# Two attention stages of a two-layer kernel rewritten: rotated state columns, sums on TensorE, roots by logarithm, named activation tables, fewer filling matmuls, new buffers and a new order

## The chip, the core and the metric

The kernel runs on one core of one Trainium2 chip. The engines are called PE (TensorE; PEld is its weight load), DVE (VectorE), ACT (ScalarE), POOL (GpSimd) and SP (SyncE, here only an issuer of DMAs). The metric is the device time of one execution in microseconds (us); the median of several runs is compared.

## What is computed

Two transformer layers in float32 over 8 x 512 tokens of width 128. Each layer is an attention of a recurrent kind and a mixture of experts; each has a layer norm ahead of it and a residual around it.

```python
# layer 0: state per head (16 heads of 8), for every token
kk = kt[..., :, None] * kt[..., None, :]
state = state * (1.0 - bb * kk) + bb * (vt[..., :, None] * kt[..., None, :])
out_t = jnp.einsum('bhij,bhj->bhi', state, qt)     # q and k have length 1
...
logits = relu(x @ rw1 + rb1) @ rw2 + rb2           # 8 experts, top 2, at most 512 tokens each
# layer 1: gated linear attention (16 heads, keys of 4, values of 8)
gk = log_sigmoid(h @ gk_w1 @ gk_w2 + gk_b2) / 16
S = exp(gt)[..., None] * S + kt[..., None] * vt[..., None, :]
o = _rms(einsum('bhk,bhkv->bhv', qt, S), rms_w) * (g * sigmoid(g))
x = x + o @ Wo; x = x + gelu(_ln(x) @ W1 + b1) @ W2 + b2
...                                                # 16 experts, top 4, all tokens kept
```

## The kernel before, in words

The work comes in five stages, in the profile one after the other: **attention 0** (0 to 396 us), **experts 0** (to 480), **attention 1** (to 826), **experts 1** (to 1035) and the **output**.

The 8 sequences of 512 tokens are the batches b. A recurrence is run by DVE as a prefix scan along the tokens: 128 partitions are (head, row of the state), and one instruction scans four columns of the state, 128 x 2048 elements. Attention 0 has 8 columns, so two scans (groups g = 0 and 1) for a batch; attention 1 has 4 columns, one scan.

`attend0(b)` (L440) normalizes x (`affine`, L412, with a square root on ACT and a reciprocal on DVE, `statistics`, L423), transposes it on PE, projects it to keys, queries, values and gate, finds the norms of the heads by squares and a matmul (L584 to L600), and scales keys, queries and values. Keys and queries go to DRAM through SP's queue (L551, L557) and come back spread over the partitions, four columns for a transfer of 1 MB (`broadcasts`, L470, also on SP): `add` tiles for the keys, `qb` for the queries. Then for each group (L639 on): DVE multiplies keys by the row's key (`dec`, L643, 128 x 2048), ACT turns that into 1 - kk (`decay`, L621, L623), DVE multiplies by the value (L649), scans (L655) and multiplies by the queries (L659); PE sums the columns and centres them (`summing`, L626, L632, 8 matmuls of 512 columns for a batch). A root and a reciprocal (`deviation`, L673), the gate and the output projection follow. `route(b)` (L713) finds the two experts of each token and scatters the token's row to DRAM, one indirect DMA of POOL per 128 tokens and choice (L836). `fills` (L852) clears the DRAM areas, `later_constants` (L877) loads the expert weights `ew1_all` and `ew2_all` on SP during the whole stage.

`attend(b)` (L1080) is the like for layer 1: the two expert results are added to x on DVE (L1095), statistics and two roots (L1101, L1102), projections; keys and queries go out as `pairs` (L1160), the decays as `decays` (L1218), and `spread_rows` (L1140) brings them back as `kb`, `qb_both` and `gb_both`. The decay is exp((min(z,0) - ln(1 + exp(-|z|))) / 16), made by ACT with three table changes and by DVE (L1203 to L1215). A scan (L1232), a product with the queries, 16 matmuls that sum and transpose (L1245), a root mean square (L1253 to L1258), the gate, the output matrix, a second layer norm and an MLP with GELU follow. `residual` (L1108) adds the bias b2 to x on POOL (L1117). `route1(b)` (L1327) picks 4 of 16 experts and scatters each token four times (L1449, 16 indirect DMAs for a batch).

Experts 1 works on 144 tiles of 128 rows in 36 quads of four: `fetch` (L1583) loads the rows on SP, `prepare` (L1590) transposes them on PE and copies the expert's first weights out of `fw1` with an address read from a register (DVE, L1599), `first` (L1602) and `second` (L1619) are the two matmuls with GELU between; `second` reads the weights of `fw2` with an address read by PE (L1628). POOL scatters each tile (L1638). The output adds the four results of a token (L1674, L1676).

The order inside both attention stages is made by a small planner when the program is written (`Order`, L93 to L166): each batch is a set of chains that say which engine they want next and for how long, each with a rank (its batch; the routes get `b + BEHIND`); the planner takes the step that can begin first, then the lower rank. Tiles come from rings with a number of buffers (L332 on), a chain waits until one is given back. On the chip each engine then runs its instructions strictly in the planned order. Where the planner sees PE idle for longer than `FILL` (0.35), it puts in filling matmuls of 128 columns that write to a bank nobody reads (`fill`, L896, L898), one for each 0.35 us. A switch of the activation table is planned as 1.3 us; the loads themselves are put in by the builder.

Of the kernel before, what the change touches and what calls it, by code (L numbers as in the profile page):

```python
# [17 lines left out]
P = 128  # L18
B = 8
# [19 lines left out]
NC1 = I1 // P  # L39

# [22 lines left out]
PE, DVE, ACT, POOL, SP = "PE", "DVE", "ACT", "POOL", "SP"  # L63
HOP = 0.2
SWITCH = 1.3
FILL = 0.35
# [25 lines left out]

class Order:  # L93
# [6 lines left out]
    def __init__(self):  # L100
        self.engines = {}
        self.table = None
        self.fill = None
        self.chains = []
        self.now = 0.0
# [14 lines left out]
    def settle(self):  # L120
        moved = True
        while moved:
            moved = False
            for c in sorted(self.chains, key=lambda c: c[:2]):
                want = c[5]
                if isinstance(want, Signal):
# [17 lines left out]
    def run(self):  # L144
        self.settle()
        while self.chains:
            best = None
            for c in self.chains:
# [6 lines left out]
                switch = len(want) > 2 and self.table not in want[2].split("|")  # L155
                key = (start + (SWITCH if switch else 0.0), c[0], c[1])
                if best is None or key < best[0]:
                    best = key, c, engine, us, want[2].split("|")[0] if switch else self.table
            assert best is not None, "chains wait for each other"
            key, c, engine, us, self.table = best  # L160
            gap = key[0] - self.engines.get(engine, 0.0)
            if engine == PE and self.fill is not None and gap > FILL:
                self.fill(int(gap / FILL))
            c[2] = self.engines[engine] = key[0] + us
# [6 lines left out]
def two_layers(ctx: ExitStack, tc: tile.TileContext, a: dict, out: bass.AP):  # L171
# [7 lines left out]
    stage = ExitStack()  # L179

# [8 lines left out]
    def load(name, shape, src, queue=nc.gpsimd):  # L189
        t = const.tile(shape, F32, name=name)  # L190
        queue.dma_start(t, src)
        return t
# [6 lines left out]
    wk0 = load("wk0", [P, C], a["L0_attn_Wk"], nc.scalar)  # L199
    wq0 = load("wq0", [P, C], a["L0_attn_Wq"], nc.scalar)  # L200
    wb0 = load("wb0", [P, NH], a["L0_attn_Wbeta"], nc.scalar)
    wv0 = load("wv0", [P, C], a["L0_attn_Wv"], nc.scalar)
    wg0 = load("wg0", [P, C], a["L0_attn_Wg"], nc.scalar)
# [15 lines left out]
    center = const.tile([P, P], F32, name="center")  # L219
    nc.vector.tensor_scalar_add(center, ident, -1.0 / C)  # L220

    head_sum = const.tile([P, NH], F32, name="head_sum")
    nc.vector.tensor_reduce(head_sum, ident.rearrange("p (h d) -> p h d", d=D), AX.X, ALU.add)
    spread = const.tile([3 * NH, 3, P], F32, name="spread")
    for i in range(3):
# [4 lines left out]
        )  # L230
    number1 = const.tile([P, E1], F32, name="number1")
# [7 lines left out]
    first0 = const.tile([P, E0], F32, name="first0")  # L239
# [22 lines left out]
    wout0 = load("wout0", [P, C], a["L0_attn_Wout"])  # L262
    rw1 = load("rw1", [P, H0], a["L0_ffn_rw1"])
    rw2 = load("rw2", [P, NC0, E0], a["L0_ffn_rw2"].rearrange("(c p) e -> p c e", p=P))
    rb2 = load("rb2", [P, E0], a["L0_ffn_rb2"].partition_broadcast(P))
# [10 lines left out]
    ps = bank_ring.idle[0][2]  # L276
    nc.tensor.transpose(ps[:, :NCOLS], rows, ident[:NCOLS, :NCOLS])
    nc.vector.tensor_copy(cols, ps[:, :NCOLS])

    def col(at, n=P):  # L280
        return cols[:n, at : at + 1]


    wout_g = const.tile([P, C], F32, name="wout_g")
    nc.vector.tensor_scalar_mul(wout_g, wout0, col(LNG0))
    wout_b = const.tile([P, C], F32, name="wout_b")
    nc.vector.tensor_scalar_mul(wout_b, wout0, col(LNB0))
    rmsw2 = const.tile([P, 1], F32, name="rmsw2")
    nc.vector.tensor_scalar_mul(rmsw2, col(RMSW), 0.5)
# [5 lines left out]
    nc.vector.memset(empty, 0.0)  # L295
    nc.gpsimd.iota(
        empty[:, :, DEST : DEST + 1].bitcast(I32), [[0, 1], [0, 1]], base=NA0, channel_multiplier=0
    )
# [3 lines left out]
    zeros = const.tile([P, 2 * C], F32, name="zeros")  # L302
# [8 lines left out]
    ew1_all = experts.tile([P, E0, H0], F32, tag="first", name="ew1_all")  # L311
# [34 lines left out]
    h_ring = ring(work, 1, [P, NC0, S], "hT")  # L346
    pick = [P, NT, 2, E0]
    FLIGHT0 = 4
    BEHIND = 2
    finished = [0]  # L350

    class Small0:
# [1364 lines left out]
```

## Time and profile before

| what | us |
|---|---|
| median of 3 runs | 1061.47 (1058.1 to 1071.24) |
| the profiled execution | 1068.49 |
| its span, first to last instruction | 1066.7 |
| first scan of attention 0, last one | 51.5, 343.8 |
| first scan of attention 1, last one | 538.9, 720.6 |
| first scatter of attention 1, last one's start | 626.6, 822.5 |
| scatters of experts 1 | 841.3 to 1028 |
| mean granted PE clock | 0.854 |

A timeline line gives start and length in us, engine, line, operation, output<-inputs and shape; in brackets the idle time of the engine ahead of it and what ended it. A line of stretches gives start:end, length, then for PE, PEld, DVE, ACT and POOL the busy time and instructions, the granted PE clock, the busy share of the DMA engines and GB/s. A line of groups gives line, engine, operation, tiles and count, then busy time in us and mean in ns, then idle time ahead. A float32 matmul leaves two PE records; counts of matmuls in the text are counts in the program.

### The profile page before, as it was taken

To read this page: it belongs to the slowest core of one execution; us is meant where nothing else is said; L and a number is where in the kernel's file an instruction comes from. 1 tells how busy PE (TensorE), PEld (TensorE's weight loads), DVE (VectorE), ACT (ScalarE), POOL (GpSimd) and SP (SyncE) were. 2 spreads that over 40 slices of the span, in tenths; PEclk is the share of its full clock that TensorE was granted. 3 is DMA by queue.
4 is the path that set the end of the run, shared out by engine and by line. 5 is a ranking of instruction groups with operands and counts; after the bars stand their busy time and mean duration, and the time that the engine had idled before them with its cause. 6 is when DMAs were issued, how large, how long until landed. Compare 5 with 4: busy or idle time off the path is not lost. (4 is left out here: it accounts for less than half of the span.)

```text
span 1066.7 us, 15813 instructions
## 1 busy us (share of the span) xinstructions
PE 824.1 (77%) x4783; PEld 632.3 (59%) x4783; DVE 648.2 (61%) x1553; ACT 472.3 (44%) x900; POOL 475.5 (45%) x459
## 2 busy tenths in 40 slices
PE   6989799999888949987658986797880899888500
PEld 5756566666655734463557664677770899777400
DVE  5477886876897511118379987697552465544217
ACT  3734464473424403426424785454630455444200
POOL 9000013612316441542000138887776377777753
PEclk8887997886988968998869997889995899999855
DMA  7965854867533002016774447642511344432138
GB/s 173 229 150 128 197 141 116 199 181 189 148 84 92 5 9 78 22 49 170 191 174 108 113 121 182 157 117 66 180 52 50 91 126 119 119 98 78 51 126 272
DMA packets 81684, 132.08 MB, mean 124 GB/s; under 512 B 13044, under 2 KB 58998, under 8 KB 74432
## 3 DMA queue, kind: packets, MB, share of 16 engines
q1 hardware_dynamic: 61824, 100.86, 37.7%
q0 software_dynamic: 14832, 27.84, 9.1%
q10 hardware_dynamic: 4944, 2.37, 0.8%
q8 instruction: 39, 0.64, 0.3%
q14 instruction: 45, 0.37, 0.1%
HBM read 94.79 MB, written 41.14 MB: 127 GB/s over the span
## 5 line engine op out<-in xcount | busy, mean ns | idle before, releaser
L836 POOL DMA_INDIRECT row<-rows,si x64 | 91.2, 1426 | 270.6 <-DVE kT L614 148.9
L1449 POOL DMA_INDIRECT rows<-rows,si x128 | 151.9, 1187 | 57.1 <-issue 33.6
L1638 POOL DMA_INDIRECT res<-qy,to x144 | 143.2, 994 | 61.4 <-issue 33.6
L898 PE MATMUL idle_bank<-ones,ident 128*128 128x128 f32 x1216 | 166.9, 294 | 2.3 <-POOL ident masks.py:199 1.5
L898 PEld LDWEIGHTS idle_bank<-ones,ident 128*128 128x128 f32 x1216 | 159.1, 209 | 13.3 <-issue 10.2
L1617 ACT ACTIVATE qh<-mid,cols 128x128 f32<-128x128 f32 x288 | 85.9, 367 | 78.1 <-PE mid L1609 69.9
L1609 PE MATMUL mid<-dT,qw 128*128 128x128 f32 x576 | 73.2, 281 | 18.4 <-DVE dT L1600 18.4
L632 PE MATMUL acc<-add,center 128*128 128x512 f32 x128 | 67.3, 674 | 21.7 <-DVE add L659 21.4
L1609 PEld LDWEIGHTS mid<-dT,qw 128*128 128x128 f32 x576 | 68.3, 194 | 23.1 <-DVE dT L1600 23.1
L655 DVE TENSOR_TENSOR_SCAN add<-dec,add 128x2048 f32<-128x2048 f32 x16 | 70.8, 4424 | 0.6
L1628 PE MATMUL qyp<-fw,qh 128*128 x576 | 71.0, 276 | 0.0
L1117 POOL TENSOR_TENSOR x<-x,b 128x512 f32<-128x512 f32 x8 | 11.8, 1480 | 127.0 <-DVE u L1112 100.7
L1628 PEld LDWEIGHTS qyp<-fw,qh 128*128 128x128 f32 x576 | 67.5, 192 | 0.6 <-issue 0.2
L1599 DVE COPY qw<-fw 128x256 f32 x144 | 45.1, 315 | 34.4 <-DMA rows<-rows,si 17.8
L632 PEld LDWEIGHTS acc<-add,center 128*128 128x128 f32 x128 | 26.3, 216 | 53.6 <-issue 28.4
L1245 PE MATMUL acc<-ident,kb 128*128 128x128 f32 x256 | 35.1, 303 | 23.3 <-DVE gb_both L1230 21.7
L955 POOL DMA_INDIRECT res<-y,de x32 | 31.0, 969 | 46.9 <-DVE dT L928 22.0
L659 DVE TENSOR_TENSOR add<-add,qb 128x2048 f32<-128x2048 f32 x16 | 36.6, 2288 | 22.6 <-DMA qb<-queries 22.3
L1245 PEld LDWEIGHTS acc<-ident,kb 128*128 128x128 f32 x256 | 34.0, 218 | 24.1 <-DVE gb_both L1230 21.9
L623 ACT ACTIVATE dec<-dec 128x2048 f32<-128x2048 f32 x16 | 30.5, 1908 | 28.8 <-DVE dec L643 28.8
L1594 PE MATMUL qT<-ident,de 128*128 128x128 f32 x144 | 24.2, 284 | 23.0 <-DMA de<-rows 23.0
L1635 DVE TENSOR_TENSOR to<-de,nowhere 128x4 int32<-128x4 int32 x36 | 5.9, 163 | 58.7 <-DMA res<-qy,to 55.1
(335 smaller groups left out, 1752.5 us busy)
## 6 DMA issues: line engine op xcount, KB each, us to landing
add<-keys SPq DMA_DIRECT2D x16, 1024.0 KB
qb<-queries SPq DMA_DIRECT2D x16, 1024.0 KB
de<-rows SPq DMA_DIRECT2D x144, 65.0 KB
kb<-pairs SPq DMA_DIRECT2D x8, 1024.0 KB
qb_both<-pairs SPq DMA_DIRECT2D x8, 1024.0 KB
gb_both<-decays SPq DMA_DIRECT2D x8, 1024.0 KB
yk<-res SPq DMA_DIRECT2D x8, 1024.0 KB
res<-zeros POOLq DMA_DIRECT2D x8, 512.0 KB
```

The costliest lines, as they stand in the source:

```text
L632: nc.tensor.matmul(acc, lhsT=center, rhs=st[:, j, :], start=g + j == 0, stop=(g + 1) * J + j == D + J - 1)
L655: nc.vector.tensor_tensor_scan(flat, dec.rearrange("p j t -> p (j t)"), flat, 0.0, ALU.mult, ALU.add)
L659: nc.vector.tensor_mul(st, st, q_j)
L836: nc.gpsimd.indirect_dma_start(out=row0_w[(b * NT + t) * 2 + k], out_offset=bass.IndirectOffsetOnAxis(ap=m.si[:, t, k : k + 1], axis=0), i ...
L898: nc.tensor.matmul(idle_bank[:, 0:P], lhsT=ident, rhs=ones, start=True, stop=True)
L1245: nc.tensor.matmul(chunk(acc, t), lhsT=chunk(st[:, j, :], t), rhs=ident, start=j + t == 0, stop=j + t == DK + NT - 2)
L1449: nc.gpsimd.indirect_dma_start(out=rows1_w[(b * NT + t) * K1 + k], out_offset=bass.IndirectOffsetOnAxis(ap=m.si[:, t, k : k + 1], axis=0), ...
L1599: nc.vector.tensor_copy(w1_q[:, i, :], fw1[:, bass.ds(at, I1)])
L1609: nc.tensor.matmul(mid[c][:, here], lhsT=w1_q[:, i, c * P : (c + 1) * P], rhs=dT[:, here], start=True, stop=True)
L1617: nc.scalar.activation(hT[:, c, here], mid[c][:, here], AF.Gelu, bias=cols[:, bass.ds(at + c, 1)])
L1628: nc.tensor.matmul(ps[:, here], lhsT=hT[:, c, here], rhs=fw2[:, bass.ds(at + c * C, C)], start=c == 0, stop=c == NC1 - 1,)
L1638: nc.gpsimd.indirect_dma_start(out=res1_w[4 * q + i], out_offset=bass.IndirectOffsetOnAxis(ap=to[:, i : i + 1], axis=0), in_=y[:, i, :], i ...
```

## The change

It touches both attention stages, experts 1 and the planner.

- Attention 0, state columns: each tile of keys is written to DRAM twice, one after the other for each head, so that a partition (head, i) can read the four columns from column i + 4g on, wrapping round. The decay 1 - k_i k_c is symmetric, so three of the four decays of group 1 are those of group 0 in other rows: PE moves them with the permutation matrices `turned` and ACT copies them; DVE multiplies only one column of group 1 (512 elements instead of 2048). Queries are written and read in the same way.
- Roots: 1 / sqrt(v + eps) is now exp(-0.5 ln(v + eps)) on ACT (`inverse_root`), without a reciprocal on DVE, everywhere in both stages.
- Tables: steps name a whole table set (`EXP`, `GELU`, `SILU`), and the planner puts in the load itself (`order.load`).
- Sums on PE: in attention 1 the additions of expert results, of u, of b2 and of the two halves of the decay become matmuls with the identity that add up in PSUM, and the statistics read PSUM; ACT copies the sums to SBUF. POOL no longer adds b2. The rows for the scatter are normalized once and then copied four times per 128 tokens, into six small buffers where there were two of a whole batch.
- Stores of keys, queries, pairs and decays are issued by ACT, not SP. In attention 1 the queries' broadcast is issued behind that of the decays.
- Fillings: only for planned gaps of over 2.5 us, one wide matmul (512 columns, zeros) per us: 29 in the program, where there were 608 narrow ones.
- Buffers in attention 0: `add` 4 (3), `dec` 3 (2), `qb` 4 (2). The `qb` buffers take the room of the expert weights, which are therefore loaded after the last scan. The fills of DRAM begin after the first scan. The matrix of constants is transposed later. In attention 1 there are 4 banks (5) and 3 sums (2).
- Order: ranks are lists of numbers (`TURN0`, `REST0`, `ROUTE0`, `TURN`, `TURN_REST`, `TURN_ROUTE`), a batch changes its rank after its scan, and the planned lengths of steps are changed.
- Experts 1: the biases of the first layer lie beside the expert's weights, and DVE also copies the second weights, so PE and ACT read no addresses there; one of four row loads is issued by ACT.

The activation table loads in the built program are 24 in attention 0 (33 before), 38 in attention 1 (39), 1 in experts 1 (1).

The diff, cut to its core:

```diff
-FILL = 0.35
+FILL = 1.0
+PAUSE = 1.5
...
-            if engine == PE and self.fill is not None and gap > FILL:
-                self.fill(int(gap / FILL))
+            if table is not None:
+                self.table = table
+                self.load(table)
+            if engine == PE and self.fill is not None and gap > PAUSE + FILL:
+                self.fill(int((gap - PAUSE) / FILL))
...
+    order.load = nc.scalar.preload_act_table_set
-    a_ring = ring(work, 3, [P, J, S], "add")
-    d_ring = ring(work, 2, [P, J, S], "dec")
-    b_ring = ring(work, 2, [P, J, S], "qb")
+    a_ring = ring(work, 4, [P, J, S], "add")
+    d_ring = ring(work, 3, [P, J, S], "dec")
+    b_ring = Ring([t[:, i] for t in (qb_first, qb_second) for i in range(2)])
...
+    TURN0 = [-47.0, -20.5, -9.0, 3.5, 25.0, 10.0, 52.0, 111.0]
+    REST0 = [-12.0, -3.0, -100.0, -3.5, -74.0, 38.5, 21.5, -29.5]
+    ROUTE0 = [10.0, 12.5, 29.5, 55.0, 13.0, 46.0, 39.0, 42.0]
...
+    def inverse_root(dst, src, **of):
+        nc.scalar.activation(dst, src, AF.Ln, **of)
+        nc.scalar.activation(dst, dst, AF.Exp, scale=-0.5)
...
+                    bass.AP(every.tensor, every.offset + g * J * S, [[2 * D * S, NH], [S, D], [1, J * S]]),
...
+        def send(dst, src):
+            for r in range(2):
+                nc.scalar.dma_start(dst.rearrange("(h r j) t -> r h j t", r=2, j=D)[r], src)
...
-            nc.sync.dma_start(keys[b], kT)
+            send(keys[b], kT)
...
-        def decay(dec, done):
-            yield ACT, 1.93
-            nc.scalar.activation(dec, dec, AF.Identity, bias=1.0, scale=-1.0)
+        def decay(g, n):
+            yield ACT, 0.49 * n
+            nc.scalar.activation(decs[g][:, :n, :], decs[g][:, :n, :], AF.Identity, bias=1.0, scale=-1.0)
+            if g == 0:
+                decayed[0].set(order.now)
+                return
+            yield decayed[0]
+            for r in range(J - 1, 0, -1):
+                ps = yield bank_ring
+                yield PE, 0.93
+                nc.tensor.matmul(ps, lhsT=turned[:, r, :], rhs=decs[0][:, r, :], start=True, stop=True)
+                if r == 1:
+                    used_dec()
+                yield ACT, 0.6
+                nc.scalar.copy(decs[1][:, J - r, :], ps)
+                bank_ring.give(order.now, ps)
+            decayed[1].set(order.now)
...
-            yield DVE, 0.57 * J
-            nc.vector.tensor_mul(dec, st, by_j(kT))
+            n = J if g == 0 else 1
+            yield DVE, 0.57 * n
+            nc.vector.tensor_mul(dec[:, :n, :], st[:, :n, :], by_j(kT, n))
...
+    TURN = [-10.5, 6.0, 8.5, 11.5, 11.5, 16.0, 24.5, 10.0]
+    TURN_REST = [-35.5, -33.0, 6.5, 3.0, -73.0, -24.0, 81.0, 9.0]
+    TURN_ROUTE = [-7.5, -41.5, 1.0, -4.0, -17.0, 17.0, 8.5, -15.0]
...
-        for k in range(2):
-            yield DVE, 0.7
-            nc.vector.tensor_add(x_b, x_b, ys[:, :, k, :])
+        px = yield acc_ring
+        yield PE, 2.7
+        for i, part in enumerate((x_b, ys[:, :, 0, :], ys[:, :, 1, :])):
+            nc.tensor.matmul(tiled(px), lhsT=ident, rhs=part, start=i == 0, stop=i == 2)
...
-        yield ACT, 0.6, "sqrt"
-        nc.scalar.activation(m.rs["u"][:, 0, :], m.mv["u"][:, :, 1], AF.Sqrt, bias=eps)
-        nc.scalar.activation(m.rs["u"][:, 1, :], m.mv["u"][:, :, 1], AF.Sqrt, bias=eps2, scale=1.0 + EPS)
+        yield ACT, 0.8, EXP
+        inverse_root(m.rs["u"][:, 0, :], m.mv["u"][:, :, 1], bias=eps)
+        inverse_root(m.rs["u"][:, 1, :], m.mv["u"][:, :, 1], bias=eps2, scale=1.0 + EPS)
...
-            yield POOL, 1.3
-            nc.gpsimd.tensor_add(x_b, x_b, b2.unsqueeze(1).to_broadcast([P, NT, C]))
...
-            nc.sync.dma_start(pairs[b], kq)
+            nc.scalar.dma_start(pairs[b], kq)
...
+        for t in range(NT):
+            rw = yield rows_ring
+            yield ACT, 1.0
+            nc.scalar.copy(rw[:, :, 0:C], xr[:, t : t + 1, :].to_broadcast([P, K1, C]))
+            nc.scalar.copy(rw[:, :, WEIGHT], m.ex[:, t, :])
+            order.add(TURN_ROUTE[b], scatter(t, rw))
...
+            nc.vector.tensor_copy(w1_q[:, i, :], fw1[:, bass.ds(at, WE)])
+            nc.vector.tensor_copy(w2_q[:, i, :], fw2[:, bass.ds(at, I1)])
```

## The prediction

> **What bounds the kernel now.** I read the page's busy shares first, then the busy time of each engine in the five stages, the fillings alone, and then inside the two changed stages the timelines of POOL, DVE and ACT.
>
> ```profile
> span 1066.7 us, 15813 instructions
> PE 824.1 (77%) x4783; PEld 632.3 (59%) x4783; DVE 648.2 (61%) x1553; ACT 472.3 (44%) x900; POOL 475.5 (45%) x459
> ```
> No engine is full over the span, so the stages decide. Here they are (attention 0; experts 0; attention 1; experts 1; output); behind each stretch: its length, then busy time of PE, PEld, DVE, ACT, POOL, the granted clock, the DMA share, GB/s.
> ```profile
> 0.00:396.00 396.00, 343.50 (x1617) 239.72 (x1617) 280.38 (x585) 180.70 (x276) 122.89 (x131) 0.84 0.56 137
> 396.00:480.00 84.00, 75.08 (x276) 41.51 (x276) 10.49 (x16) 28.77 (x41) 31.36 (x33) 0.93 0.18 50
> 480.00:826.00 346.00, 250.95 (x1594) 204.07 (x1594) 241.99 (x678) 175.68 (x294) 165.01 (x144) 0.85 0.50 129
> 826.00:1035.00 209.00, 154.52 (x1296) 146.99 (x1296) 91.35 (x252) 87.19 (x289) 143.19 (x144) 0.91 0.35 95
> 1035.00:1067.00 32.00, 0.00 (x0) 0.00 (x0) 23.99 (x24) 0.00 (x0) 13.05 (x8) 0.50 0.84 283
> ```
> The same for the filling matmuls alone (PE, PEld): 69 of the 343 us and 89 of the 251 us of PE are fillings, so real PE work is 275 and 162 us.
> ```profile
> 0.00:396.00 396.00, 68.69 (x478) 65.36 (x478) 0.84 0.56 137
> 480.00:826.00 346.00, 88.60 (x654) 84.33 (x654) 0.85 0.50 129
> ```
> In attention 0 DVE sets the pace: 280 us of work, and what stops it is a transfer or another engine for a few us at a time, such as the queries here. In attention 1 the first half is a chain of small waits; DVE, in order, even stands behind a store that SP issued late:
> ```profile
> 64.27 2.29 DVE L659 TENSOR_TENSOR add<-add,qb 128x2048 f32<-128x2048 f32 x1 [6.95 <-DMA qb<-queries]
> 531.56 1.40 DVE L1205 TENSOR_SCALAR gk<-bank,cols 64x512 f32<-64x512 f32 x2 [11.62 <-DMA decays<-gk]
> ```
> The second half of attention 1 and all of experts 1 are POOL's scatters, one every 1.28 us, back to back:
> ```profile
> 609.28 1.28 POOL L1117 TENSOR_TENSOR x<-x,b 128x512 f32<-128x512 f32 x1 [17.12 <-ACT rows L1340]
> 626.63 1.07 POOL L1449 DMA_INDIRECT rows<-rows,si  x1 [15.96 <-DVE ex L1391]
> 628.01 0.97 POOL L1449 DMA_INDIRECT rows<-rows,si  x1 [0.30 <-issue]
> 642.11 4.66 POOL L1449 DMA_INDIRECT rows<-rows,si  x1 [0.30 <-issue]
> ```
> ```profile
> L1449 POOL DMA_INDIRECT rows<-rows,si x128 | 151.9, 1187 | 57.1 <-issue 33.6
> L1638 POOL DMA_INDIRECT res<-qy,to x144 | 143.2, 994 | 61.4 <-issue 33.6
> ```
> From 626.6 to 823.5 the 128 scatters take 197 us: 128 x 1.28 = 164, some 26 for those stretched beside DVE's wide operations (mean 1.187 against the usual 0.98), a few us of adds and waits. So attention 1 ends at "first scatter + 197", and what counts is when the first scatter starts.
>
> **Attention 0.** DVE: eight of sixteen decay products shrink from 2048 columns (2.29) to 512 (0.68): -12.9. The reciprocals go: the 128x128 one 8 x 0.95 = 7.6, the small ones about 3. Sum -23.5. PE: 24 wide permuting matmuls at 1.05 (67.3 us / 64 at L632) are +25; the fillings go from 69 us to 19 wide ones, about 20. PE busy 343 becomes 320. ACT: 9 table loads fewer (33 to 24) -11.5; eight decays of 1.91 become 0.6, -10.4; 24 copies out of PSUM +14; second halves of the roots, 24 x 0.3 = +7; 32 stores (each column tile goes out twice) are issued by ACT at 0.44, +14: 181 becomes 194. Behind such a store stand ACT's next activations, 0.9 us each time; SP is rid of them.
>
> Between the first and last scan (51.5 to 343.8, 292 us) the DVE rows in the order before sum to 235, in the new order to 219. At the same share, 0.806, the stretch takes 272: -20. The four qb buffers (two before) and the order that puts batch 1 between batch 0's steps attack the 22.3 us that DVE waits for qb; against that the second scan of a batch now waits for ACT, PE and ACT (0.6 + 3 x 1.05 + 0.6), which no row shows. Bounds: nothing gained on waits and PE at its limit, 0; all qb waits gone too, -42. I take -20 and 5 for the start (first wait of 6.95 gone, zeros for the fillings come at 11.2 by POOL and eight wide fillings stand before the first transpose, which costs some of it): **-25**. The tail behind the last scan (48 us) keeps its chain. The expert weights, 4 MB, now load there: at 4.3 us per MB (what the broadcasts need) 17 us beside a DMA share of 0.03. Without that cover experts 0 would start late by up to 17. Experts 0 otherwise: **0**.
>
> **Attention 1, start.** The loads by name fail at one place: in the built order, ACT loads a table 16 times by itself for the first four batches' logarithms and exponentials, so the stage has 38 loads, 39 before. The row's price:
> ```profile
> 511.14 1.28 ACT L1210 ACT_TABLE_LOAD   x1
> 512.44 1.15 ACT L1210 ACTIVATE za<-za 64x512 f32<-64x512 f32 x2
> ```
> 1.28 us, with 0.02 to the activation behind it. Before the first normalized tile there are eight such loads and eight 0.3 us activations, so it begins at 496 where it was 487; the first keys go out at 514 (495 before), the first decays at 522 (525). But gb now goes out ahead of qb, and stores don't wait behind SP's broadcasts, so the first scan starts at 532 (525 + store 2.2, 1 MB 4.3), not 538.9.
>
> The page "ScalarE: Activation LUTs", section "What ACT_TABLE_LOAD costs", counts 2.66 us for a switch, with a drain. The trace has 1.28 and no drain beside it. By the page those eight loads would cost 21 us, attention 1 would begin 11 later than by the row, and the sum below would be -34 in place of -45.
>
> **Attention 1, to the first scatter.** Four scans are over at about 586, as before (585). Then batch 0's route comes ahead of later batches: the DVE work ordered between the first scan and its weights is 55 us, ACT's from the first decays on 52. From 532 and 522 that is 587 without a wait; with 11 for waits (squares, root, product and transpose each change the engine) 598, first scatter 600, 26 before the 626.6. POOL's x + b adds (8 x 1.48), which stood in front of it waiting for later batches, are gone; their work is on PE. In the train: 32 iotas at 0.3 instead of 8 and four adds, +2.
>
> Does supply last? From one route to the next DVE has 18 to 25 us of work, ACT 17 to 26, POOL 22 with its iotas. ACT rises from 176 to 225 us (copies from PSUM, row copies 32 x 0.6 in place of 0.8, issues), DVE falls from 242 to 199 (adds 11.9 + 5.4 + 5.4, gate steps 5.7 + 5.2, reciprocals 8, copies), PE's real work rises from 162 to 230 (56 wide at 1.05, 32 small at 0.27). All are under 300. The statistics now read PSUM, which no row shows for them; products with a PSUM operand take 0.68 as those without do, so 0. The ring of banks shrinks from 5 to 4 and that of sums grows from 2 to 3; its waits are in the lower bound. ACT's row copies wait for six small buffers, and everything else of ACT behind them, but only while POOL has six tiles (31 us) before it. Bounds: first scatter no earlier than before and 8 us of gaps, +8; first scatter at 587 with no gap, -40. I take **-22**.
>
> **Experts 1.** DVE gains 144 copies of 0.315, 45 us: per quad 2.5 + 1.3 and 0.6 of address reading (now 11.4 us of gaps for 144 copies, then twice as many), 4.4, under POOL's 4 x 1.28 = 5.1, so POOL hides it; beyond 5.1 each 0.1 would cost 36 x 0.1 = 3.6. The first quad's scatter comes later by its four copies. ACT's 36 loads (0.33) have room beside 2.4 us of activations per quad. **+2**, at most +10. Output: 0.
>
> Sum: -25 - 22 + 2 = -45. The profiled execution took 1068.5 (span 1066.7 and 1.8 around it): 1023.5. It is 7.0 above the median, 1061.5, so the forecast for the median is **1016.5**.
>
> **Rivals.** (1) Attention 1 gains nothing: ACT, 225 us in order with 16 loads at its head, delivers the first rows at 626 again. For: ACT's growth; against: its work ordered up to there is only 52 us. 1061.5 - 25 + 2 = 1038.5.
>
> (2) The waits go as well: -42 and -40, which gives 981. For: most DVE stops in the first stage are qb or ACT; against: PE then runs at 320 of 354 us.
>
> (3) Slower, by the PE clock. The fillings kept it up; behind an idle stretch it is halved:
> ```profile
> 510.00:520.00 10.00, 10.00 (x86) 9.52 (x86) 5.78 (x4) 9.39 (x13) 0.00 (x0) 1.00 0.91 207
> 530.00:540.00 10.00, 0.00 (x0) 0.00 (x0) 2.53 (x4) 0.00 (x0) 0.00 (x0) 0.50 0.83 201
> 540.00:550.00 10.00, 4.26 (x20) 4.26 (x21) 9.92 (x4) 0.00 (x0) 0.00 (x0) 0.50 0.55 127
> ```
> The page "TensorE: Matmul & The Clock Gate", section "Why this matters for your kernels", warns of gaps over about 3 us, and the trace agrees (idle from 524 on, 0.50 in the 530s). The change removes fillings, which the rule speaks against.
> Price: at a clock of 0.65 in attention 0 PE's 320 us become 320 x 0.84 / 0.65 = 413, the stage about 430, +34; attention 1 +5: 1100. It decides below about 0.72, where PE's 373 us equal my 371 us stage. Against: real work fills 80% of that stage, so gaps are short.
>
> **How the numbers follow.** Likeliest 57%, own range 1000 to 1035; rival 1 13%; rival 2 20%; rival 3 10%. The range 968 to 1050 leaves half of rival 3 and the ends of rival 2 out. Two per cent (21 us; the runs lie 13 apart) is about what a measurement tells from no change: faster means under 1040, so most of the likeliest, rival 2 and half of rival 1: 0.78; same 0.13; slower 0.09.
>
> **What would show it.** Right: first scan of attention 0 near 48 and the last near 320; first scatter of attention 1 near its start + 120 and the train still 197; 16 loads there in the first 45 us; experts 1 at 5.1 per quad. Wrong: granted clock under 0.75 in attention 0, POOL gaps of over 5 us inside the train, DVE waits on decay tiles above 20 us in total.

## The result and the profile after

The changed kernel takes 1062.65 us (median of 20 runs, 1058.57 to 1070.67), the kernel before 1061.53 (20 runs): a ratio of 1.0009, interval 0.9986 to 1.0033. The forecast was 1016.5 (range 968 to 1050), and nothing was gained. The profiled execution took 1060.58, its span:

```profile
span 1058.9 us, 13577 instructions
```

Two views say where the expected 45 us went. The first has a line for each of the three trains that set the stages: duration of one (lowest, median, highest), then the start of the first and of the last. Before, in the order scans of attention 0, row scatters of attention 0, scatters of attention 1:

```profile
L655 DVE TENSOR_TENSOR_SCAN add<-dec,add x16: 4423/4425/4426, 51.5 to 343.8; 128x2048 f32<-128x2048 f32 x16
L836 POOL DMA_INDIRECT row<-rows,si x64: 967/972/4119, 155.6 to 395.4; - x64
L1449 POOL DMA_INDIRECT rows<-rows,si x128: 972/983/4925, 626.6 to 822.5; - x128
```

And after:

```profile
L724 DVE TENSOR_TENSOR_SCAN add<-dec,add x16: 4424/4425/4425, 51.6 to 349.6; 128x2048 f32<-128x2048 f32 x16
L909 POOL DMA_INDIRECT row<-rows,si x64: 977/984/4857, 200.6 to 408.7; - x64
L1563 POOL DMA_INDIRECT rows<-rows,si x128: 976/984/4674, 614.0 to 816.6; - x128
```

The last row scatter marks the end of attention 0; it moved from 395.4 to 408.7. With the same marks for the other stages (last result scatter of experts 0 at 473.3 and 487.3, of experts 1 at 1027.1 and 1020.3):

| stretch | before | after | change | forecast |
|---|---|---|---|---|
| attention 0, to its last row scatter | 395.4 | 408.7 | +13.3 | -25 |
| experts 0 | 77.9 | 78.6 | +0.7 | 0 |
| attention 1, head: to its first scatter | 153.3 | 126.7 | -26.6 | -26 |
| attention 1, train: first to last scatter | 195.9 | 202.6 | +6.7 | +2 to +4 |
| experts 1 | 204.6 | 203.7 | -0.9 | +2 |
| output | 39.6 | 38.6 | -1.0 | 0 |

The sum is -7.8, between one profile that lies 7 above its median and one that lies 2 below; the medians differ by +1. So the forecast failed in attention 0, by 38 us, and by a few in the train. The second view shows how: what DVE waited for from 40 to 405 us (total, times, longest), the four longest rows.

```profile
DVE og L768 <- ACT sq L752: 17.7, 4, 11.1
DVE lg L849 <- PE acc L835: 11.3, 4, 4.7
DVE x L780 <- ACT rs_o L460: 10.6, 2, 10.3
DVE add L733 <- DMA qb_first<-queries: 10.5, 3, 7.6
```

The first row before was the queries' transfer:

```profile
DVE add L659 <- DMA qb<-queries: 22.3, 5, 6.9
```

Now it is ACT: all its rows together are 55.8 us, 21.0 before. DVE's own work did fall (280 to 261 us), but ACT came late. And what ACT waited for, after (two rows) and before (one):

```profile
ACT rows L802 <- DMA row<-rows,si: 49.0, 10, 11.7
ACT dec L691 <- PE bank L687: 36.9, 21, 6.1
```

```profile
ACT rows L729 <- DMA row<-rows,si: 10.9, 6, 3.0
```

ACT stands 49 us (10.9 before) until a row buffer comes free from its scatters, and 37 us for the permuting matmuls, in order, with all its later work behind it.

One more thing has to be said before the experiments. Most of them belong to sets of runs in which the kernel before takes 1165 to 1179 us, not 1062. A stage mark up to the first scatter of attention 1 is the same there (after_again: 409.4 and 126.0 behind experts 0, against 408.7 and 126.7), while the train and experts 1 are longer (236 and 252). So early marks are compared across sets, and times only as ratios to the kernel before in the same set. In one such set the changed kernel has 0.985 (0.978 to 0.992), not 1.00; the slower profile of the kernel before (before_again) has a train of 243 us, longer than the 236 of the changed kernel, where the first profiles have 196 and 203. The other sets have no run of the changed kernel, so small differences of ratios between sets say little.

How far does an early mark vary by itself? In seven profiles with the changed kernel's order of DVE's and ACT's instructions in attention 0, its end lies at 408.2 to 415.2; in five with one other order (that of experiment 5) at 388.6 to 400.8. A shift of 3 us is within that; the two ranges do not meet.

And a caution on the experiments: an edit that changes a step or a buffer makes the planner order the whole stage anew. DVE's order differs from the changed kernel's from 197 us on in experiment 1 and from about 80 us on in experiments 2 and 3. Experiments 4 and 7 and the two runs named "same order" hold it still, and none of the edits in attention 0 touches the order of attention 1.

### The profile page after: what moved, and what is told of

The parts are those of the page before. It is cut to its first block, busy times and chain, and to the rows that moved or that the text cites. A ratio compares the mean times of both kernels' runs of the same rounds, so it can differ in the third digit from the quotient of the medians.

```text
span 1058.9 us, 13577 instructions
## 1 busy us (share of the span) xinstructions
PE 800.4 (76%) x3849; PEld 526.9 (50%) x3849; DVE 620.1 (59%) x1589; ACT 491.7 (46%) x1077; POOL 467.3 (44%) x475
## 5 line engine op out<-in xcount | busy, mean ns | idle before, releaser
L1748 ACT ACTIVATE qh<-mid,qw 128x128 f32<-128x128 f32 x288 | 79.2, 378 | 91.0 <-PE mid L1742 89.1
L701 PE MATMUL acc<-add,center 128*128 128x512 f32 x128 | 72.3, 720 | 13.4 <-DVE add L733 13.2
L1759 PE MATMUL qyp<-qw,qh 128*128 128x128 f32 x576 | 70.0, 275 | 0.0
L1731 DVE COPY qw<-fw 128x258 f32 x144 | 45.9, 319 | 37.0 <-DMA rows<-rows,si 23.5
L1759 PEld LDWEIGHTS qyp<-qw,qh 128*128 128x128 f32 x576 | 67.1, 192 | 0.0
L701 PEld LDWEIGHTS acc<-add,center 128*128 128x128 f32 x128 | 29.2, 235 | 55.5 <-issue 34.5
L1807 DVE TENSOR_TENSOR x<-x,yk 128x512 f32<-128x512 f32 x24 | 24.1, 1014 | 28.3 <-DMA yk<-res 27.1
L802 ACT ACTIVATE rows<-x,sh,rs 128x256 f32<-128x256 f32 x32 | 17.5, 596 | 49.0 <-DMA row<-rows,si 49.0
L985 PE MATMUL idle_bank<-zeros,ident 128*128 128x512 f32 x58 | 30.5, 665 | 12.4 <-POOL zeros L335 11.6
L822 PE MATMUL bank<-xT,rw 128*128 128x512 f32 x64 | 38.8, 735 | 1.4 <-ACT xT L814 1.4
```

Source lines behind the costliest of these rows:

```text
L701: nc.tensor.matmul(acc, lhsT=center, rhs=st[:, j, :], start=g + j == 0, stop=(g + 1) * J + j == D + J - 1)
L1731: nc.vector.tensor_copy(w1_q[:, i, :], fw1[:, bass.ds(at, WE)])
L1748: nc.scalar.activation(hT[:, c, here], mid[c][:, here], AF.Gelu, bias=w1_q[:, i, I1 + c : I1 + c + 1])
L1759: nc.tensor.matmul(ps[:, here], lhsT=hT[:, c, here], rhs=w2_q[:, i, c * C : (c + 1) * C], start=c == 0, stop=c == NC1 - 1,)
```

## The experiments

**1. A third row buffer in attention 0.**

```diff
-    rows_ring = ring(work, 2, [P, NT, 2, W1], "rows")
+    rows_ring = ring(work, 3, [P, NT, 2, W1], "rows")
...
-            self.tmp = t("tmp", pick)
+            self.tmp = self.hot
```

> The changed kernel with three row buffers in attention 0 in place of two (room for it from one 64-column tile of the route that shares another's place). Buffer theory: attention 0 gained nothing because ACT, in order, stood 49 us behind its two row buffers until the scatters had landed, and every activation, decay and copy behind it stood too. Then that wait falls below 20 us, the last scan of attention 0 comes near 325 in place of 349.6, and the run takes about 1040. PE theory: attention 0 is at TensorE's limit (92 to 100% busy from 160 to 300), the wait only changes its name; the last scan stays within 340 to 350, the run takes 1058 to 1063.

Measured: 0.9687 (0.9619 to 0.9755) of the kernel before. The wait for row buffers is gone (49 to 0 us) and the last row scatter comes at 406.6, 2 earlier; the last scan comes later (355.9). The buffer theory, with the last scan near 325, falls. Where the wait went is seen in the stretches from 260 to 340 (length, then busy time of PE, PEld, DVE, ACT, POOL; granted clock):

```profile
260.00:300.00 40.00, 40.00 (x147) 28.31 (x147) 25.51 (x71) 18.36 (x33) 14.84 (x11) 0.71 0.56 140
300.00:340.00 40.00, 36.59 (x109) 19.55 (x108) 29.91 (x69) 13.80 (x23) 30.47 (x20) 0.74 0.32 81
```

ACT waits for PE instead: 119 us from 40 to 405, 94 in the changed kernel. PE is full in the first stretch, at a clock of 0.71; the changed kernel has 39.0 of 40 there, at 0.79. Of the 36.6 in the second stretch 14.5 are filling matmuls (2.8 of 22.4 in the changed kernel), so real work fills little more than before. This was read as a limit of PE, and PE was tested next.

**2. Without the permuting matmuls.** The kernel leaves out the turning: ACT copies the decays as they stand, in the wrong rows.

```diff
-                ps = yield bank_ring
-                yield PE, 0.93
-                nc.tensor.matmul(ps, lhsT=turned[:, r, :], rhs=decs[0][:, r, :], start=True, stop=True)
...
-                nc.scalar.copy(decs[1][:, J - r, :], ps)
+                nc.scalar.copy(decs[1][:, J - r, :], decs[0][:, r, :])
```

> The changed kernel without the 24 wide permuting matmuls: ACT copies the second half's decay columns from the first half's tile as they stand, so the decays are not turned to the right column (that part of the computation is left out). PE theory: TensorE's 25 us were what took the gain of attention 0; the run takes about 1040 with the last scan near 325. Buffer theory: the wait for row buffers stays near 49 us, the run takes 1055 to 1063.

Measured: 0.9658 (0.9596 to 0.9721). Last scan 336.5, last row scatter 393.0: 16 earlier, with ACT's copies still there, in a new order.

**3. The decay products back on DVE**, which is the same without leaving anything out.

```diff
-            n = J if g == 0 else 1
+            n = J
...
-            for r in range(J - 1, 0, -1):
...
+            decayed[g].set(order.now)
```

> The changed kernel with all eight decay products made on DVE again, as before: no permuting matmuls, no copies out of PSUM, DVE 8 x 1.6 = 13 us more. PE theory: the 24 permuting matmuls (29 us at the granted clock) lengthen attention 0 by more than DVE's 13 us are worth, because PE is 92 to 100% busy from 160 to 300; the end of attention 0's scatters comes 10 to 16 earlier than 409.7 and the run is 1 to 1.5% faster than the changed kernel. DVE theory (that of the prediction): DVE sets the pace, the stage gets 10 longer, the run 1% slower.

> Decay products on DVE, two row buffers, once more, beside the same with three buffers on one chip. Two-limits theory: end of attention 0's scatters near 399 again and 6 to 12 later than with three buffers. Rival: the buffers add nothing once the turning is gone; both end within 4 us of each other.

Measured: 0.9729 (0.966 to 0.9797) and, in another set, 0.9736 (0.9688 to 0.9784). The end of attention 0 is at 399.3 and 396.8; 10 and 13 earlier although DVE has 13 us more to do. So DVE's amount of work is not what made the changed kernel's stage long. How much of the time DVE is busy between the starts of the first and the last scan (the third of the busy times) is seen in the kernel before, the changed kernel and here (unturned, unturned_2):

```profile
51.50:343.80 292.30, 263.08 (x1177) 175.40 (x1177) 233.76 (x382) 134.64 (x200) 73.85 (x51) 0.85 0.61 150
```

```profile
51.60:349.60 298.00, 259.19 (x960) 151.52 (x960) 219.67 (x390) 134.31 (x239) 69.99 (x58) 0.83 0.62 155
```

```profile
51.80:331.60 279.80, 244.02 (x897) 139.31 (x897) 226.71 (x349) 128.20 (x210) 69.34 (x56) 0.84 0.65 165
```

```profile
48.20:331.60 283.40, 244.60 (x894) 139.91 (x892) 226.84 (x351) 129.12 (x211) 69.64 (x56) 0.83 0.66 165
```

That is a share of 0.80 before, 0.74 with the turning, 0.81 and 0.80 without it. The order is new here too, so a luckier order is a rival. Against it: three different orders with the turning (the changed kernel, experiments 1 and 6) have the last scan at 349.6, 355.9 and 377.8; three without the matmuls (experiments 2, 3 and 5) at 336.5, 331.6 and 326.8 to 332.5.

**4. Each permuting matmul twice**, order unchanged.

```diff
+                for _ in range(2):
-                nc.tensor.matmul(ps, lhsT=turned[:, r, :], rhs=decs[0][:, r, :], start=True, stop=True)
+                    nc.tensor.matmul(ps, lhsT=turned[:, r, :], rhs=decs[0][:, r, :], start=True, stop=True)
```

> The changed kernel with each of the 24 permuting matmuls of attention 0 issued twice into the same bank, the order of everything else unchanged. PE theory: PE is 92 to 100% busy over most of the stage, so a second set costs about what taking the first away gave (16) up to its whole time (29): end of attention 0's scatters at 425 to 438 in place of 409.7, the run 1.4 to 2.5% slower than the changed kernel. Rival: ACT's wait for row buffers paces the stage and the second set is hidden in it; end at 410 to 415, the run the same.

Measured: 1.0056 (1.0027 to 1.0085), in a set in which the kernel before takes 1062: half a per cent over the changed kernel's 1.0009, with intervals that overlap. The end of attention 0 is at 412.4, 3 later, which lies within what that mark does by itself. So the time that PE spends on the turning is not what it costs. The groups show where the second set went; the summing and the permuting matmuls (busy, mean ns of one), here

```profile
L702 PE MATMUL acc<-add,center 128*128 128x512 f32 x128 | 67.1, 676 | 9.1 <-DVE add L734 8.8
L688 PE MATMUL bank<-dec,turned 128*128 128x512 f32 x96 | 49.1, 641 | 0.7 <-ACT dec L692 0.7
```

and in the changed kernel (after_again):

```profile
L701 PE MATMUL acc<-add,center 128*128 128x512 f32 x128 | 72.5, 722 | 13.5 <-DVE add L733 13.3
L687 PE MATMUL bank<-dec,turned 128*128 128x512 f32 x48 | 28.0, 675 | 0.7 <-ACT dec L691 0.7
```

The permuting group grew by 21 us (28.0 to 49.1), but PE's busy time from 40 to 400 only by 14 (306.9 to 320.6), at a clock of 0.83 in place of 0.80. ACT's two waits trade: 46.6 for turned columns and 36.2 for row buffers, 82.8 together, where the changed kernel's first profile has 85.9. So the size of ACT's wait for turned columns is no price either: it grew by 10 and the stage did not. What is left of the turning is that ACT has to wait for PE at all in the middle of its queue, and the order that is made around these steps. The runs do not part these two.

**5. Both edits, three buffers and DVE's products.**

> Both edits at once: all eight decay products on DVE (no permuting matmuls) and three row buffers in attention 0. Theory of two limits in series: three buffers alone changed nothing because PE, at 92 to 100%, was the next limit (the last scan even came 6 later), and without the permuting matmuls the last scan came 18 earlier but the end of the scatters only 10, because the routes still waited for buffers behind it. Together the last scan comes near 330 and the last scatter 52 behind it as in the kernel before: end of attention 0 at 382 to 386 in place of 409.7, the run 2 to 2.5% faster than the changed kernel. Rival: the tail is bound by the chain of the routes itself; the end stays at 396 to 402, the run 1 to 1.2% faster.

> Decay products on DVE and three row buffers. Two-limits theory: end of attention 0's scatters 6 to 12 earlier than with two buffers, the run 0.6 to 1% faster than that one. Rival: within 4 us, the runs the same.

Measured: 0.9705 (0.9618 to 0.9792) and 0.962 (0.9553 to 0.9687). The first profile ended attention 0 at 388.6, which looked like the two limits in series; side by side in one set it does not hold. Two buffers (unturned_2) and three (unturned_rows3_2):

```profile
L893 POOL DMA_INDIRECT row<-rows,si x64: 979/985/4682, 152.3 to 396.8; - x64
```

```profile
L893 POOL DMA_INDIRECT row<-rows,si x64: 980/986/4116, 151.9 to 396.3; - x64
```

The buffers add nothing to the stage; 388.6 is the lowest of five profiles with the same order, the others lie at 394.5 to 400.8. In the ratios the two-buffer and the three-buffer kernel differ by 1.2% in that set, with intervals that just miss each other; no stage mark up to the first scatter differs (601.7 in both), so that is not a gain of attention 0. It lies in the train, 252 and 239 us, and is not explained.

**6. The old ranks in attention 0.**

```diff
-    TURN0 = [-47.0, -20.5, -9.0, 3.5, 25.0, 10.0, 52.0, 111.0]
+    TURN0 = [float(b) for b in range(B)]
...
-    ROUTE0 = [10.0, 12.5, 29.5, 55.0, 13.0, 46.0, 39.0, 42.0]
+    ROUTE0 = [float(b + 2) for b in range(B)]
```

> The changed kernel with the three lists of ranks of attention 0 replaced by what the kernel before has: batch number for the attention steps, batch number plus 2 for the route. Order theory: the new lists put routes ahead of later batches' attention steps and so ACT behind the row buffers; with the old ranks ACT's wait for them falls to about 15 us and the run takes 1040 to 1050. Rival: the lists spread work better than turns by batch do; without them the stage is longer, run 1070 to 1080.

Measured: 0.9864 (0.9805 to 0.9922), in a set without the changed kernel; attention 0 ends at 427.2, 18 later, with no wait for row buffers. DVE's first wait there:

```profile
DVE dec L722 <- ACT dec L691: 36.4, 7, 10.8
```

It is the rotated chain: the second scan of a batch waits for ACT, PE and ACT. In the new order that wait is 7.2, while ACT has its 49 us at the row buffers; that the one is the price of the other is likely, not shown.

**7. The old fillings.**

```diff
-FILL = 1.0
-PAUSE = 1.5
+FILL = 0.35
+PAUSE = 0.0
...
-            nc.tensor.matmul(idle_bank, lhsT=ident, rhs=zeros, start=True, stop=True)
+            nc.tensor.matmul(idle_bank[:, 0:P], lhsT=ident, rhs=ones, start=True, stop=True)
```

> The changed kernel with the fillings of the kernel before (128 columns wide, one for every 0.35 us of idle PE that the recording foresees, from the start). Clock theory: every real matmul of attention 0 took 7 to 8% longer than before (720 ns in place of 674 for those of the summing) because less filling lowers the granted clock; with the old fillings they take 680 again, the 313 us of real PE work fall by 20, and the run is 1 to 2% faster than the changed kernel. Rival: the fillings are work for PE as well, in order ahead of real matmuls, and the clock is lower because PE now has more real work; then the run is the same or up to 2% slower.

Measured: 0.9795 (0.9718 to 0.9872) against 0.985 (0.978 to 0.992): not told apart. Attention 0 ends at 410.0 and its summing matmuls take 715 ns, within the 709 to 746 of the other profiles in this order; the granted clock from 40 to 400 is 0.82, against 0.80 in the changed kernel and 0.84 before. The time is as the rival has it. But the planner sees less idle time here: from 40 to 400 it put in 85 fillings (170 records) where the kernel before has 206, so the full set was not tried.

**8. The changed kernel and the kernel before once more.**

> The changed kernel as it stands, beside the kernel before on this chip, because the chip of the first four experiments took 1165 us for the kernel before in place of 1061. If the ratio does not depend on the chip it is 1.00; if the changed kernel's later stages suffer less there, 0.97.

> A second profile of the kernel before, since its first one took 7.0 us more than its median. If the stages of that profile are typical, attention 0 ends at 396, experts 0 takes 78 and the first scatter of attention 1 comes 152 behind it; if the 7 us lie in one of these stages, it is that much shorter here, and the gain that the comparison of profiles shows for it is smaller.

Measured: 0.985 (0.978 to 0.992) for the changed kernel. The kernel before, 1159.1 in one run, has its last row scatter at 394.3 and its first scatter of attention 1 151.9 behind experts 0. So the two early stages of the first profile were typical (395.4 and 153.3), and the 7 us that it lies over its median are not in them.

**9. The first named load of attention 1 put where it holds.** Where attention 1's first load by name was meant to stand, the changed kernel's trace has none, and tables were loaded one function at a time:

```profile
499.54 0.30 ACT L459 ACTIVATE rs_u<-mv_u,eps 128x4 f32<-128x4 f32 x1 [16.79 <-DVE mv_u L1167]
499.86 1.28 ACT L460 ACT_TABLE_LOAD   x1
501.15 0.20 ACT L460 ACTIVATE rs_u<-rs_u 128x4 f32<-128x4 f32 x1
501.36 1.28 ACT L459 ACT_TABLE_LOAD   x1
```

```diff
+        nc.scalar.preload_act_table_set(EXP)
         results0(E0 - 1)
...
+    order.table = EXP
```

> The changed kernel with the first named table load of attention 1 put at the end of experts 0, behind its last activations, where it can't be moved ahead; the 16 loads that the program put in by itself at the head of attention 1 are gone. Load theory: ACT is 95 to 99% busy from 500 to 540, so 16 x 1.28 = 20 us of it leave the path to the first scatter: first scatter some 15 earlier than 126 behind the start of the stage, the train of 203 unchanged, run about 1048. Rival: the first scatter is held by the first 1 MB broadcasts (DMA share 1.0 from 550 to 590) and PE; it comes at most 4 earlier, the run takes 1058 to 1063.

Measured: 1.0082 (1.0047 to 1.0116). The head took 118.8 in place of 126, half of the 15 expected, but the train 277 in place of 236: with one load less in its reckoning the planner had put the whole stage in another order, and the scatters waited for rows (61.9 us in four waits). So it was run again with the order kept:

```diff
-    order.load = nc.scalar.preload_act_table_set
+    loads = []
+    order.load = lambda name: loads.append(nc.scalar.preload_act_table_set(name) if loads else name)
```

> The changed kernel with the first named load of attention 1 at the end of experts 0, as in the third run, but with every other instruction left in the changed kernel's order (in that run the recording had shifted by one load and ordered the whole stage anew). Load theory: from the end of experts 0 to the first scatter 118 in place of 125.7, as in that run, and the train of scatters as long as the changed kernel's on this chip (236), so the run is 0.7% faster than the changed kernel. Rival: the train starts earlier but waits for its rows, and ends where it did; the run is the same.

Measured: 0.9687 (0.96 to 0.9774). Head 112.3, train 238.5. The same place on ACT:

```profile
506.06 0.20 ACT L460 ACTIVATE rs_u<-rs_u 128x4 f32<-128x4 f32 x1
506.17 0.28 ACT L459 ACTIVATE rs_u<-mv_u,eps 128x4 f32<-128x4 f32 x1
```

Of 16 x 1.28 = 20.5 us of loads, 14 come off the head; eleven profiles that keep the loads and this order up to the first scatter have heads of 125.9 to 129.1. That it reaches the end is seen in one set of runs: the four runs with it and experiment 5's edits (1111.75 to 1122.9, experiment 11) all lie below the four with experiment 5's edits alone (1125.37 to 1136.26).

**10. The number fills of the train on DVE**, first freely ordered, then in the changed kernel's order.

```diff
+    numbers = small.tile([P, B * NT * K1], I32, tag="numbers", bufs=1, name="numbers")
+    nc.gpsimd.iota(numbers, [[P * K1, B * NT], [1, K1]], base=0, channel_multiplier=K1)
...
-            nc.gpsimd.iota(
-                rw[:, :, DEST].bitcast(I32), [[1, K1]], base=(b * S + t * P) * K1, channel_multiplier=K1
-            )
+            nc.vector.tensor_copy(rw[:, :, DEST].bitcast(I32), numbers[:, (b * NT + t) * K1 : (b * NT + t + 1) * K1])
```

> The changed kernel with the 32 small number fills in POOL's scatter train of attention 1 (0.17 us each and 0.28 to the scatter behind it) replaced by DVE copies of 128x4 integers out of a table made once. POOL theory: POOL is the bound from the first scatter of attention 1 on, so 32 x 0.45 = 14 us leave the train of 203; the run is 1.2% faster than the changed kernel. Rival: POOL stands for rows and scans as much as for its own work (28 us of gaps and 26 of stretched scatters); the copies come late behind DVE's scans, and the run is the same within 0.5%.

> The 32 number fills of attention 1's train on DVE as before, out of a table made once, but every other instruction in the changed kernel's order. POOL theory: 32 x 0.45 = 14 us leave the train. On a chip like the first (train 203, with no wait for rows) it takes 189, the run 1.3% faster than the changed kernel. Rival, and what the chips of the last calls suggest (train 236, of it 36 us of waits for rows on top of the 0.3 behind each scatter): the train waits that much longer for its rows, and the run is the same within 0.5%.

Measured: 0.9893 (0.9856 to 0.9929), train 242.7; and, where the kernel before takes 1062, 1.0044 (1.0006 to 1.0082), train 198.8 in place of 202.6, but the first scatter 4.7 later in its stage. Of the 14 us only 4 left the train, and they were lost ahead of it. About 2 of the 4.7 arise where the first copy stands in DVE's queue; the other 3 were there before any copy and are within what a head does by itself. Not a gain.

**11. The two edits that helped, together:** decay products on DVE and the named load in its place (the three buffers came along).

> The edits of the two runs above in one kernel: decay products on DVE, three row buffers, first named load of attention 1 at the end of experts 0. If the parts add, end of attention 0 near 384, first scatter of attention 1 at 581 in place of 614, and the run 2.7 to 3.2% faster than the changed kernel. If the train waits for rows, 2 to 2.5%.

> The kernel with the decay products on DVE, three row buffers and the first named load of attention 1 at the end of experts 0 once more. If the gain of the two heads reaches the end, as on the other chips (0.9581 of the kernel before, where the changed kernel had 0.985), it takes 0.973 of the kernel before on a chip like the first, about 1033; if the train of scatters gives it back there, 0.99 or more.

> The same with the first named load of attention 1 at the end of experts 0. Load theory: head of attention 1 (end of experts 0 to first scatter) 112 to 114 in place of 126, and 1% faster than the kernel without it. Rival: the train gives it back, the same.

Measured: 0.9581 (0.9483 to 0.9679), 0.9559 (0.9494 to 0.9623) and 0.9588 (0.9528 to 0.9648) of the kernel before; the changed kernel has 0.985 in its set. Heads 114.6, 114.7 and 114.0. In such sets this kernel beats the kernel before by 4% and the changed kernel by about 3%. In a set in which the kernel before takes 1062 it was not run.

## Why the prediction was wrong

**Attention 0 (forecast -25, measured +13.3).** By the marks, the 38 us missed lie in three places:

| part | forecast | measured |
|---|---|---|
| start, to the first scan (51.5, 51.6) | -5 | 0 |
| first scan to last scan (292.3, 298.0) | -20 | +5.7 |
| last scan to last row scatter (51.6, 59.1) | 0 | +7.5 |

The step that failed is "at the same share, 0.806, the stretch takes 272". DVE's work in that stretch was forecast well (219, measured 219.7; before 233.8), and the queries' wait did shrink (22.3 to 14.8). But DVE's share fell to 0.74. Without the turning it is 0.80 to 0.81, as before: the share rule broke with the work that was moved from DVE to a chain through ACT and PE.

- The turning was priced as 25 us of PE (it took 28 to 29) and as three short hops in DVE's wait, to which the sum gave nothing. Without it the stretch takes 280 to 283 in place of 298 though DVE has 13 us more to do, and the stage ends 10 to 16 earlier (experiments 2 and 3); with PE's part doubled it ends no later than the mark varies (experiment 4). That the turning costs this is shown as far as three orders with it and three without it can show it; how, as a wait in ACT's queue or by the order made around it, is open.
- "The tail behind the last scan keeps its chain" was wrong. It is 7.5 longer in the changed kernel, and 14 to 16 without the turning (65 to 68), where the scans end 8 to 12 ahead of the kernel before and the last row scatter comes no sooner (397 to 399 against 394 to 395). What goes with it is the number of row scatters still to be done when the last scan starts: 24 of 64 in the kernel before, 30 in the changed kernel, 32 in experiment 3; 16 in experiments 1 and 6, whose tails are 51 and 49. So scans that end earlier leave more of the routes behind them. What sets the pace of that tail is not settled; a third row buffer did not change it (experiment 5).

The start gained nothing: the first scan stands where it stood. The wait for row buffers was thought of in attention 1, where it did not come (2.3 us), and not in attention 0, where it did. It looked like the cause, but without it the end came only 2 earlier (experiment 1, in a new order). And the signs of being wrong that the prediction named did not show this: DVE's waits on decay tiles are 7.2 us (it named 20) and the clock is 0.82 (0.75). The cost stood in ACT's waits, which it had not listed.

**Attention 1, head (forecast -26, measured -26.6).** Right in size, and for the reasons given: the first scan comes 56.9 behind experts 0 (forecast 58.7) and the first scatter 69.8 behind that (68). The 16 loads came, at 1.28 each. The head then took the time that the sum gave by the trace's row. The Trainium skill's page "ScalarE: Activation LUTs", section "What ACT_TABLE_LOAD costs", has that 1.28 for the load too, but with the drain it counts 2.66 for a switch; as an estimate, that would have made the head 11 longer, and no run here shows it. Experiment 9 shows what the loads hid: without them 14 more would have come.

**Train (forecast +2 to +4, measured +6.7).** The 32 number fills were priced at 0.3. One costs its 0.16 and 0.28 ahead of the scatter behind it:

```profile
618.91 0.16 POOL L1558 IOTA rows<- 128x4 int32 x1
619.35 1.00 POOL L1563 DMA_INDIRECT rows<-rows,si  x1 [0.28 <-POOL rows L1558]
```

By these rows that is 14 us, against 8 fills and four additions before. Taking them out brought 4 (experiment 10), so they are not the whole account of the train. One gap of 5.8 us, where the prediction named 5 as a sign of being wrong, was there as well.

**Experts 1 (+2, measured -0.9), experts 0 and output (0, measured +0.7 and -1.0)**: right; POOL hides the 144 copies at 5.2 a quad (36 quads from 834.1 to 1020.3), as reckoned.

**The rivals.** "Attention 1 gains nothing" is refuted by the head. "The waits go as well" is refuted: the queries' wait went down by 8 and ACT's went up by 35. The clock rival had its sign right (0.80 in place of 0.84 from 40 to 400, the summing matmuls 7% longer) but not its size (0.65). Whether the missing fillings are the cause stays open: experiment 7 put less than half of them back and moved the clock to 0.82.

## What to carry to other kernels

When an in-order engine's work falls because it moves to other engines, don't scale the stage by the first engine's share: first list what the other engines will wait for, above all an engine that is made to wait for another in the middle of its own queue. Test a suspected limit from both sides, since taking the permuting matmuls away and doubling them gave different answers (16 and 3 us), and only both together show that it is not PE's time that counts. Where a planner makes the order, an edit changes two things at once; hold the order still, or compare several orders. The size of a wait is not what taking it away brings: 49 us of waits for row buffers went, and the stage ended 2 earlier. A load by name may not stand where the program asked for it: look for it in the trace.

## What was not expected of the hardware

The same kernels took 1062 us in some sets of runs and 1165 to 1179 in others, with equal marks up to some 600 us. Whether the chip decides is not shown: the record has chip number 2 both at a set with 1062 and, 400 s later, at one with 1179. In experts 1, with the same order, one matmul of the first product took 279 ns in the changed kernel's first profile and 305 in a slower set (rows3), where PE stood 20.9 us for nothing that the profile shows:

```profile
L1742 PE MATMUL mid<-dT,qw 128*128 128x128 f32 x540 | 68.3, 279 | 19.1 <-DVE dT L1733 19.1
```

```profile
L1742 PE MATMUL mid<-dT,qw 128*128 128x128 f32 x544 | 84.0, 305 | 34.4 <-issue 20.9 <-DVE dT L1733 13.2
```

The cause is open.

The granted clock from 40 to 400 does not follow from how busy PE is. In the changed kernel's order, 24 added matmuls went with a rise from 0.80 to 0.83 and with summing matmuls 6% shorter (722 to 676 ns). But in other orders PE busy for 329 us has 0.79 (experiment 1), and PE busy for 297 us has 0.84 (unturned_2).
